# Transposing attention probabilities and MLP tokens: by TensorE, or by VectorE in blocks and a trip through DRAM

## The chip, the cores and the metric

The kernel runs on one core of one Trainium2 chip. The metric is the device time of one execution in microseconds; the time of a kernel is the median of its runs. One further execution is taken by the hardware profiler, and every duration of a single instruction comes from that one.

## The reference

The input `x` holds 8 images of 192 channels and 64 x 64 pixels, in float32. Two layers follow each other; all weights are float32 too.

```python
# layer 0, on tokens (one per pixel, 192 channels)
shortcut = layer_norm(tokens)
q, k, v = windows_of_8x8(shortcut) @ qkv_w.T + qkv_b       # 6 heads of 32
attn = l2n(q) @ l2n(k).T * temperature                     # 64 x 64 for each window and head
attn = where(attn >= 16th_largest_of_the_row, attn, -100)
out = softmax(attn + relative_position_bias) @ v
x2 = shortcut + (out @ proj_w.T + proj_b)
x2 = x2 + gelu(layer_norm(x2) @ fc1_w.T + fc1_b) @ fc2_w.T + fc2_b     # 192 -> 768 -> 192

# layer 1
xf = fft2(layer_norm over channels)                        # 64 x 64, for each channel
h = gelu([xf.real, xf.imag] @ fc1_w.T + fc1_b) @ fc2_w.T + fc2_b       # 2 -> 16 -> 2
x = x + ifft2(h).real
out = x + gelu(layer_norm(x) @ mlp1_w.T + mlp1_b) @ mlp2_w.T + mlp2_b  # 192 -> 768 -> 192
```

## The kernel before

**Tiling.** An image is cut into 8 bands of 512 pixels (8 rows). Every band passes `front` (load, first norm, q, k and v), `attention` twice (two halves of four windows each), and `back` (projection, residual, first MLP). When all 8 bands of an image are in, its 192 channels go in 12 groups of 16 through the Fourier part: `forward`, two of `pointwise`, and `inverse`. Then `leave` takes each band through the second MLP, turns it back into channels and stores it. That gives 128 halves of attention and 128 MLPs: 64 in `back` (tiles whose names end in `_b`) and 64 in `leave` (`_d`).

**The two transposes.** A matmul contracts over partitions. In `attention`, the probabilities `s` come out with queries on the partitions, and the product with `v` (line 928) contracts over keys. So six 128x128 blocks of `s` are transposed by TensorE into PSUM (line 903) and evicted into `at` by ScalarE or VectorE (`copy`, line 819). In `mlp`, the normalised tokens `xa` have pixels on the partitions, and the first product (`mh`, lines 589 and 602) contracts over channels. So six transposes (`to_channels`, lines 541 and 546) go into `lc`, which is evicted into `hn`. The product `mh` is passed through GELU into `h` (line 573), and the second product `mo` (line 635) brings it back to tokens, to which VectorE adds the residual (`xy` line 996, `zt` line 1212).

**What sets the order.** The kernel is written as generators that yield steps, `op(engine, weight, ...)`. The function `issue` plays them against a clock of its own for each engine: a step has a weight (one unit stands for about 10 ns), may need buffers from a ring (`get`) and gives them back (`put`), and costs extra where TensorE changes its tile shape or ScalarE its function (`change`). At each turn `issue` takes the step that can begin first, weighed by how late its task is in the image. The instructions are recorded in that order, and each engine runs its own in that order, waiting on semaphores. So the order on every engine is fixed when the program is built, and rests on the weights. The streams are: one `front`, three attentions, two `back`, one `forward`, two `pointwise`, one `inverse` and two `leave` under way at a time; the second layer of an image runs beside the first layer of the next one. The ring `ps` has 4 buffers of two PSUM banks, `att` 5 buffers of 768 columns, `hn` 2, `ot` 1.

**SyncE** issues nearly all transfers, each band's loads of `xin` (lines 192 and 195) and its stores of `z` (lines 1226 and 1228), on one queue and in order. In the kernel before, the loop gives it no weight.

Of the kernel before, what the change touches and what calls it, by code (L numbers as in the profile page):

```python
# [8 lines left out]
FP = mybir.dt.float32  # L9
# [6 lines left out]
C = 192  # L16
CA = 128
HC = 96
HW = 64
BAND = 512  # L20
# [8 lines left out]
def op(engine, weight, mode=None, get="", put="", after=None, done=None, put_too=""):  # L29
    return engine, weight, mode, get.split(), (put + " " + put_too).split(), after, done  # L30


def issue(streams, units):

    change = {"pe": 20, "act": 130, "dve": 0, "pool": 0}
    clock = {e: 0 for e in change}
    mode = {e: None for e in change}  # L40
    units = {name: [0] * n for name, n in units.items()}
    events = {}
    live = []

    def advance(task, value):
        try:
            found = task["gen"].send(value)
            while not isinstance(found, tuple):

                new = dict(task, gen=found, queue=None)  # L50
                live.append(new)
                advance(new, None)
                found = task["gen"].send(None)
            task["op"] = found
        except StopIteration:
            live.remove(task)
            if task["queue"] is not None:
                start(task["queue"])

    def start(queue):  # L60
        if queue[0]:
            gen, place = queue[0].pop(0)
            task = {"gen": gen, "queue": queue, "urgency": 360 * place, "last": (None, 0)}
            queue[1] += 1
            task["order"] = (queue[1], len(live), place)
            live.append(task)
            advance(task, None)

    for tasks, width in streams:
        queue = [list(tasks), 0]  # L70
        for _ in range(width):
            start(queue)
    while live:
        best, ready = {}, {}
        for task in live:
            engines, weights, kind, get, put, after, done = task["op"]
            if isinstance(engines, str):
                engines, weights = (engines,), (weights,)
            free = 0
            deps = [task["last"]] if after is None else after  # L80
            deps = [d if d[0] is None or d[0] in change else events.get(d) for d in deps]
            if any(d is None for d in deps):
                continue
            short = False
            for name in set(get):
                n = get.count(name)
                if len(units[name]) < n:
                    short = True
                    break
                free = max(free, sorted(units[name])[n - 1])  # L90
            if short:
                continue
            found = []
            for engine, weight in zip(engines, weights):
                begin = max(clock[engine], free)
                for source, end in deps:
                    if source is not None and source != engine:
                        end += 30 if source == "pe" else 15
                    begin = max(begin, end)
                new = kind and mode[engine] and kind != mode[engine]  # L100
                cost = change[engine] if new else 0
                found.append((begin + cost + weight, engine, begin, cost, task, weight))

            _, engine, *rest = min(found, key=lambda f: f[0] + 40 * (f[1] == "dve"))
            ready.setdefault(engine, []).append((engine, *rest))
        for engine, found in ready.items():
            first = min(begin + cost for _, begin, cost, *_ in found) + 15
            best[engine] = min(
                [
                    (  # L110
                        begin + cost + task["urgency"] - 100 * ("ps" in task["op"][4]),
                        task["order"],
                        f,
                    )
                    for f in found
                    for _, begin, cost, task, _ in [f]
                    if begin <= first
                ],
                key=lambda v: v[:2],
            )  # L120
        choice = min(best.values(), key=lambda v: (v[2][1], v[:2]))[2]
        engine, begin, change_cost, task, weight = choice
        _, _, kind, get, put, after, done = task["op"]
        for name in get:
            units[name].remove(min(units[name]))
        end = begin + change_cost + weight
        clock[engine] = end
        if kind:
            mode[engine] = kind
        for name in put:  # L130
            units[name].append(end + 15)
        task["last"] = (engine, end)
        if done:
            events[done] = (engine, end)
        advance(task, (engine, end))
# [3 lines left out]
def kernel(  # L139
# [28 lines left out]
    def psum(name):  # L168
        return psp.tile([128, 2, 512], FP, tag="ps", name=name)


    ATT_BUFS, H_BUFS, XT_BUFS = 5, 7, 4
    units = dict(
        ps=4, xt=XT_BUFS, xn=1, qk=1, vv=2, att=ATT_BUFS, qkt=1, sm=2, ot=1, hn=2, xa=2,
        h=H_BUFS, xf=1, fa=1, fz=2, fo=1, xy=2,
    )

    xins = {}
# [371 lines left out]
    def flat(name):  # L550
        return psum(name).rearrange("p k n -> p (k n)")

    def mlp(src, nm, w1, fc1_bias, w2, then=None):

        mv = yield from statistics(src, nm)
        yield op("pool", 0, get="xa")
# [1 line left out]
        last = yield from normalized(to, pair, src, mv, nm)  # L558
        if then is not None:
            yield then()  # L560
        yield op("pe", 66, "full", get="ps hn", put="xa", after=last)
        pc = flat(f"lc_{nm}")
        to_channels(pc, pair, to)
        done = yield op(EITHER, (80, 96), put="ps")
        hn = strip("hn", 2, f"hn_{nm}")
        copy(done, hn, pc[:, :ROW])
        hs = []

        def gelu(fp, ph, last):
            yield op("act", 138, "gelu", put="ps", after=[last], done=("gelu", nm, fp))  # L570
            h = sb.tile([128, 2, BAND], FP, tag="h", name=f"h_{nm}_{fp}", bufs=H_BUFS)
            for k in range(2):
                nc.scalar.activation(  # L573
                    h[:, k].rearrange("p (t n) -> p t n", t=2),
                    ph[:, :, k * HALF : (k + 1) * HALF],
                    AF.Gelu,
                    bias=fc1_bias[:, 2 * fp + k : 2 * fp + k + 1],
                )
            hs.append(h)
# [240 lines left out]

    EITHER = ("act", "dve")

    def attention(b, i, hb):

        nm = f"{b}_{i}_{hb}"
# [69 lines left out]
        yield op("pool", 150, put="sm")  # L895
        nc.gpsimd.tensor_tensor(s, s, row(rsum), ALU.mult)  # L896

        yield op("pe", 65, "full", get="ps att", put="att")
        pt = flat(f"at_{nm}")
        for h3 in range(3):  # L900
            for p in range(2):
                k = 2 * h3 + p
                nc.tensor.transpose(
                    pt[:, k * 128 : (k + 1) * 128],
                    s[:, h3, 2 * p : 2 * p + 2, :].rearrange("p w k -> p (w k)"),
                    ident,
                )
        moved = yield op(EITHER, (80, 96), put="ps")
        at = sb.tile([128, 3, 2, 128], FP, tag="att", name=f"at_{nm}", bufs=ATT_BUFS)
        copy(moved, at.rearrange("p h a t -> p (h a t)"), pt[:, :ROW])  # L910

        if hb == 0:
            yield op("pe", 53, "v", get="ps ot", put="att", after=[moved, ("vv", b, i)], done=("ot", b, i))
            ots[b, i] = strip("ot", 1, f"ot_{nm}")
        else:
            yield op("pe", 53, "v", get="ps", put="att " + held[b, i][1], after=[moved, ("ot", b, i)])
        po = psum(f"po_{nm}")
        for p in range(2):
            for h in range(6):
# [5 lines left out]
                for to, col, q0, n in places:  # L925
                    for w2 in range(2):
                        rows = slice(64 * w2, 64 * w2 + 64)
                        nc.tensor.matmul(  # L928
                            po[to : to + 32, w2, col : col + n],
                            vv[rows, p, h * 32 : h * 32 + 32],  # L930
                            at[rows, h3, p, c * 64 + q0 : c * 64 + q0 + n],
                            start=True,
                            stop=True,
                        )
# [11 lines left out]
    def back(b, i):  # L946
# [36 lines left out]
            nc.gpsimd.tensor_tensor(xt, xt, bias2, ALU.add)  # L983

        pair = lambda t, j: xt[:, j, t * C : (t + 1) * C]
        acc, last = yield from mlp(pair, f"b{nm}", wfc1, fcb[:, 0, :], wfc2, biased)
        ready = [last, ("biased", b, i)]
        yield op("dve", 98, put="ps xt", get="xy" if i == 0 else "", after=ready)
        if i == 0:
            xys[b] = (  # L990
                sb.tile([128, 2, 2, 8, C], FP, tag="xy", name=f"xy_{b}", bufs=2),
# [203 lines left out]
    def leave(b, j):  # L1195
# [3 lines left out]
        if j == 0:  # L1199
# [4 lines left out]
        yield op("pool", 0, after=blocks + [("dc", b), ("mlp", 1)])  # L1204
        xy = xys[b][0]
        acc, last = yield from mlp(
            lambda t, q: xy[:, t, q, j, :], f"d{nm}", wmlp[0], fcb[:, 1, :], wmlp[1]
        )
        left[b] -= 1
        yield op("dve", 98, get="xa", put="ps xy" if left[b] == 0 else "ps")  # L1210
# [127 lines left out]
```

## Time and profile before

| | |
|---|---|
| median of 3 runs | 4787.68 us (4782.2 to 4788.69) |
| the profiled execution: its own time | 4796.72 us |
| the profiled execution: its span | 4794.9 us |
| TensorE busy | 4545.6 us, 95% of the span |
| TensorE weight loads | 3633.2 us, 76% |
| ScalarE busy | 2663.2 us, 56% |
| VectorE busy | 2532.9 us, 53% |
| GpSimd busy | 2364.8 us, 49% |
| queue of SyncE | 53,454 packets, 54.68 MB, 3.8% of 16 DMA engines |

The span is the time between the first and the last instruction that the profiler saw. A float32 matmul stands as two records in the trace, a transpose as one. The records of matmuls overlap: the mean duration of one is a latency, and the busy time of a group counts each moment once. In a row of a group, the last part is the time that the engine sat idle just before its instructions, and what ended most of it. The granted clock is the share of its full clock that TensorE was given; its mean was 0.979. In the page's names PE is TensorE, DVE VectorE, ACT ScalarE, POOL GpSimd and SP SyncE, and SPq is SyncE's issue of a transfer.

### The profile page before, as it was taken

What the parts mean: (1) busy time and instruction counts of PE and PEld (TensorE: products, weight loads), DVE (VectorE), ACT (ScalarE), POOL (GpSimd) and SP (SyncE); (2) the same over time, 40 slices, a digit from 0 to 9 for tenths busy, and PEclk for the clock granted to TensorE, in tenths of its full rate; (3) what the DMA queues carried; (4) which work ended last, traced back from release to release, by engine and by line L of the source; (5) the groups of instructions that cost most, each with busy time, mean ns of one, the idle gap of its engine ahead of it and who ended that gap; (6) DMA issues with size and microseconds to landing.
All of it is one profiled execution on the core that took longest, in us unless ns stands there. A gap on an engine that the chain in (4) does not pass through costs nothing.

```text
span 4794.9 us, 143562 instructions
## 1 busy us (share of the span) xinstructions
PE 4545.6 (95%) x61898; PEld 3633.2 (76%) x61898; DVE 2532.9 (53%) x10479; ACT 2663.2 (56%) x3896; POOL 2364.8 (49%) x2189
## 2 busy tenths in 40 slices
PE   6787999999999999999999999999999999999989
PEld 4676777877778776887778876788767887778768
DVE  6776656455664567454655546645556454662111
ACT  4455666446664656555655556545566456553553
POOL 6677455445544446454555545536455455451100
PEclk8888999999999999999999999999999999999999
DMA  2000000000000000000000000000000000000000
GB/s 57 11 8 12 6 9 9 21 18 6 12 9 18 18 9 9 11 21 15 6 9 17 18 12 9 9 18 15 12 9 9 24 12 9 6 5 17 9 5 24
DMA packets 54100, 63.87 MB, mean 13 GB/s; under 512 B 17583, under 2 KB 36218, under 8 KB 53466
## 3 DMA queue, kind: packets, MB, share of 16 engines
q1 hardware_dynamic: 53454, 54.68, 3.8%
q8 instruction: 487, 7.98, 0.7%
q14 instruction: 147, 1.20, 0.1%
q10 hardware_dynamic: 12, 0.00, 0.0%
HBM read 29.29 MB, written 25.17 MB: 11 GB/s over the span
## 4 chain that ended last, share of the span: by engine, by line
PE 78%; POOL 7%; DVE 7%; ACT 5%; issue 2%; SPq 0%; DMA 0%; ACTq 0%; POOLq 0%; DVEq 0%
PE mo_d L635 10%; PE mo_b L635 10%; PE mh_d L589 7%; PE fh L1099 7%; PE fo L1126 6%; PE mh_b L589 6%; PE mh_d L602 4%; PE mh_b L602 3%; POOL nrm L738 3%; PE pq L754 3%; ACT fh L1082 3%; PE pp L956 2%; PE fy L1174 2%; PE po L928 2%; PE fb L1147 2%
## 5 line engine op out<-in xcount | busy, mean ns | idle before, releaser
L1082 ACT ACTIVATE fh<-fh,ab 128x1024 f32<-128x1024 f32 x768 | 813.1, 1111 | 395.1 <-PE fh L1099 392.5
L738 POOL TENSOR_TENSOR nrm<-nrm,mhalf 128x24 f32<-128x24 f32 x128 | 558.3, 4362 | 10.7
L886 POOL TENSOR_TENSOR s<-s,top 128x768 f32<-128x768 f32 x128 | 191.6, 1496 | 724.1 <-DVE s L883 445.0
L635 PE MATMUL mo_b<-wfc,h_b 128*128 128x192 f32 x3072 | 522.4, 328 | 0.3 <-ACT fh L1082 0.2
L635 PE MATMUL mo_d<-wmlp,h_d 128*128 128x192 f32 x3072 | 516.0, 327 | 1.3 <-ACT fh L1082 1.3
L635 PEld LDWEIGHTS mo_b<-wfc,h_b 128*128 128x128 f32 x3072 | 500.4, 191 | 10.0 <-issue 3.7
L635 PEld LDWEIGHTS mo_d<-wmlp,h_d 128*128 128x128 f32 x3072 | 498.1, 190 | 11.4 <-issue 5.8
L1099 PE MATMUL fh<-fz,w1p 32*128 32x248 f32 (+1 forms) x6144 | 461.0, 404 | 20.3 <-ACT fh L1082 14.7
L1099 PEld LDWEIGHTS fh<-fz,w1p 32*128 32x128 f32 x6144 | 291.2, 186 | 149.2 <-issue 77.6
L1126 PE MATMUL fo<-fh,w2p 128*32 128x264 f32 (+1 forms) x6144 | 380.0, 383 | 7.8 <-ACT fh L1082 5.6
L589 PE MATMUL mh_b<-hn_b,wfc_a 128*128 128x256 f32 x1536 | 376.5, 392 | 10.8 <-ACT xt L819 4.8
L589 PE MATMUL mh_d<-hn_d,wmlp_a 128*128 128x256 f32 x1536 | 366.5, 386 | 0.5 <-ACT hn_d L819 0.3
L573 ACT ACTIVATE h_d<-mh_d,fcb 128x512 f32<-128x512 f32 x384 | 241.1, 686 | 214.7 <-PE mh_d L602 179.3
L589 PEld LDWEIGHTS mh_b<-hn_b,wfc_a 128*128 128x128 f32 x1536 | 283.7, 192 | 76.9 <-issue 25.8
L589 PEld LDWEIGHTS mh_d<-hn_d,wmlp_a 128*128 128x128 f32 x1536 | 283.0, 191 | 56.2 <-issue 19.1
L896 POOL TENSOR_TENSOR s<-s,rsum 128x768 f32<-128x768 f32 x128 | 200.0, 1567 | 236.6 <-DVE rsum L894 191.1
L876 DVE MATCH_REPLACE8 s<-top,s 128x64 f32<-128x64 f32 x1536 | 309.6, 209 | 0.0
L1126 PEld LDWEIGHTS fo<-fh,w2p 128*32 128x32 f32 x6144 | 185.3, 110 | 158.8 <-issue 30.2
L874 DVE MAX8 top<-s 128x8 f32<-128x64 f32 x1536 | 256.7, 208 | 51.0 <-ACT s L819 50.6
L1212 DVE TENSOR_TENSOR zt<-mo_d,xy 128x768 f32<-128x768 f32 x64 | 61.2, 957 | 413.1 <-PE mo_d L635 306.4
L878 DVE MAX8 top<-s 128x8 f32<-128x64 f32 x1536 | 265.3, 214 | 0.0
L573 ACT ACTIVATE h_b<-mh_b,fcb 128x512 f32<-128x512 f32 x384 | 241.3, 691 | 38.5 <-PE mh_b L602 27.6
(218 smaller groups left out, 8763.7 us busy)
## 6 DMA issues: line engine op xcount, KB each, us to landing
xin<-in_x SPq DMA_DIRECT2D x64, 256.0 KB
out<-z SPq DMA_DIRECT2D x64, 256.0 KB
xin<-in_x SPq DMA_DIRECT2D x128, 64.0 KB
out<-z SPq DMA_DIRECT2D x128, 64.0 KB
wfc<-in_wfc SPq DMA_DIRECT2D x1, 576.0 KB
wmlp<-in_wmlp SPq DMA_DIRECT2D x1, 576.0 KB
wfc_a<-in_wfc SPq DMA_DIRECT2D x1, 384.0 KB
wfc_b<-in_wfc SPq DMA_DIRECT2D x2, 192.0 KB
```

The lines of the kernel that those rows point to most:

```text
L573: nc.scalar.activation(h[:, k].rearrange("p (t n) -> p t n", t=2), ph[:, :, k * HALF : (k + 1) * HALF], AF.Gelu, bias=fc1_bias[:, 2 * fp + ...
L589: nc.tensor.matmul(ph[:, t, k * HALF : (k + 1) * HALF], w1[0][:, f], hn[:, t * HALF : (t + 1) * HALF], start=(first and k == 0), stop=not ...
L602: nc.tensor.matmul(ph[:, t, k * HALF : (k + 1) * HALF], w1[1][rows, f], hn[rows, BAND:ROW], start=(first and k == 0), stop=not first, skip ...
L635: nc.tensor.matmul(acc[:, j, t * C : (t + 1) * C], hs[f // 2][:, f % 2, q * 128 : (q + 1) * 128], w2[:, f, ORDER[t]], start=(f == 0 and t ...
L738: nc.gpsimd.tensor_tensor(nf, nf, mhalf[:, :24], ALU.pow)
L874: nc.vector.max(best[:, 0:8], of)
L876: nc.vector.match_replace(s2, best[:, 0:8], of, -3.0e38)
L878: nc.vector.max(best[:, 8:16], s2)
L896: nc.gpsimd.tensor_tensor(s, s, row(rsum), ALU.mult)
L1082: nc.scalar.activation(hs[hf, k], ph, AF.Gelu, bias=ab[:, 0:1])
L1099: nc.tensor.matmul(phs[k // 2][:, k % 2, cols], w1p[i][rows, hf].rearrange("p h v -> p (h v)"), fz[rows, :] if rhs is None else zu[rows, : ...
L1126: nc.tensor.matmul(po[rows, :] if i == 0 else pou[rows, :, 1 : U - 1], w2p[i][:, hf].rearrange("p a v -> p (a v)"), hs[hf, k // 2][:, k % ...
```

## The change

Probabilities of images 1 to 7 (112 of 128 halves) and the tokens of all MLPs but the 8 of image 0's `back` (120 of 128) no longer go through TensorE and PSUM. VectorE transposes 32x32 blocks within SBUF, in two instructions for a half of attention and three for an MLP. SyncE then writes the result to a DRAM tile in four transfers, one for each quarter of the partitions, so that the blocks land in their places, and reads it back in one transfer (`at`) or three (`hn`). A read waits for the landing of its writes. `hn` then holds its tokens in another order, and GELU writes `h` with an access pattern that puts them right. The product with `v` reads its columns in runs of 32. The planner gets an engine `sp` with weights of its own and arrival times, three DRAM buffers for each kind of turn, a second `ot`, and a condition between the bands of an image (`xy`). As the plan is made anew, the order of the instructions changes on all engines.

```diff
-    change = {"pe": 20, "act": 130, "dve": 0, "pool": 0}
+    change = {"pe": 20, "act": 130, "dve": 0, "pool": 0, "sp": 0}
+    arrives = {"pe": 30, "sp": 210}
...
-                        end += 30 if source == "pe" else 15
+                        end += arrives.get(source, 15)
...
-            units[name].append(end + 15)
+            units[name].append(end + (150 if engine == "sp" else 15))
...
-    ATT_BUFS, H_BUFS, XT_BUFS = 5, 7, 4
+    ATT_BUFS, H_BUFS, XT_BUFS, TURN_BUFS = 5, 7, 4, 3
...
-    def mlp(src, nm, w1, fc1_bias, w2, then=None):
+    def mlp(src, nm, w1, fc1_bias, w2, by_dma, then=None):
...
+        if by_dma:
+            ready = yield op("dve", 115, get="att rows", put="xa", after=last)
+            turned = sb.tile([128, 6, 2, 2, 32], FP, tag="att", name=f"lt_{nm}", bufs=ATT_BUFS)
+            whole = to.rearrange("p j (g k) -> p j g k", k=32)
+            for t, g, c, n in ((0, 0, 0, 6), (1, 6, 4, 2), (1, 8, 0, 4)):
+                nc.vector.transpose(
+                    turned[:, c : c + n, t].rearrange("p g j k -> p j g k"),
+                    whole[:, :, g : g + n],
+                )
+            yield op("sp", 220, put="att")
+            rows = dram.tile([C, 4, 128], FP, tag="rows", name=f"lr_{nm}", bufs=TURN_BUFS)
+            into = rows.rearrange("(g c) q n -> q c g n", c=32)
+            for q in range(4):
+                part = turned[32 * q : 32 * q + 32].rearrange("p g t j k -> p g (t j k)")
+                nc.sync.dma_start(into[q], part)
+            yield op("sp", 130, get="hn", put="rows")
+            hn = strip("hn", 2, f"hn_{nm}")
+            nc.sync.dma_start(hn[:, :BAND], rows[:CA].rearrange("c q n -> c (q n)"))
+            for t in range(2):
+                nc.sync.dma_start(
+                    hn[64 * t : 64 * t + 64, BAND:],
+                    rows[CA:, 2 * t : 2 * t + 2].rearrange("c q n -> c (q n)"),
+                )
+        else:
...
+                if by_dma:
+                    to = h[:, k].rearrange("p (g t q n) -> p t q g n", g=4, t=2, q=2)
+                    of = of.rearrange("p t (q g n) -> p t q g n", q=2, g=4)
...
+    def turned_by_dma(s, nm):
+        yield op("dve", 108, get="att turn", put="att")
+        tt = sb.tile([128, 4, 2, 3, 32], FP, tag="att", name=f"tt_{nm}", bufs=ATT_BUFS)
+        for p in range(2):
+            nc.vector.transpose(
+                tt[:, :, p].rearrange("q g h k -> q h g k"),
+                s[:, :, 2 * p : 2 * p + 2, :].rearrange("q h w (e k) -> q h (w e) k", k=32),
+            )
+        yield op("sp", 220, put="att")
+        rows = dram.tile([128, 4, 192], FP, tag="at", name=f"ar_{nm}", bufs=TURN_BUFS)
+        to = rows.rearrange("(g k) c n -> c k g n", k=32)
+        for c in range(4):
+            part = tt[32 * c : 32 * c + 32].rearrange("q g p h k -> q g (p h k)")
+            nc.sync.dma_start(to[c], part)
+        moved = yield op("sp", 45, get="att", put="turn")
+        at = sb.tile([128, 4, 2, 3, 32], FP, tag="att", name=f"at_{nm}", bufs=ATT_BUFS)
+        nc.sync.dma_start(
+            at.rearrange("q c p h k -> q (c p h k)"), rows.rearrange("r c n -> r (c n)")
+        )
...
-        yield op("pe", 65, "full", get="ps att", put="att")
...
+        if b == 0:
+            moved, keys = yield from turned_by_pe(s, nm)
+        else:
+            moved, keys = yield from turned_by_dma(s, nm)
...
-                            at[rows, h3, p, c * 64 + q0 : c * 64 + q0 + n],
+                            keys(rows, h3, p, c * 64 + q0, n),
...
-        acc, last = yield from mlp(pair, f"b{nm}", wfc1, fcb[:, 0, :], wfc2, biased)
+        acc, last = yield from mlp(pair, f"b{nm}", wfc1, fcb[:, 0, :], wfc2, b > 0, biased)
...
+        if i > 0:
+            ready.append(("xy", b))
```

## The prediction

> **What bounds the kernel now.** First the busy time of the engines and the chain that ended last, from the page of the profiled run.
>
> ```profile
> span 4794.9 us, 143562 instructions
> ...
> PE 4545.6 (95%) x61898; PEld 3633.2 (76%) x61898; DVE 2532.9 (53%) x10479; ACT 2663.2 (56%) x3896; POOL 2364.8 (49%) x2189
> ...
> PE 78%; POOL 7%; DVE 7%; ACT 5%; issue 2%; SPq 0%; DMA 0%; ACTq 0%; POOLq 0%; DVEq 0%
> ```
>
> TensorE is busy for 95% of the span and carries 78% of the chain; nobody else is above 56%. So work taken from TensorE shortens the run, unless TensorE waits for what replaces it. Its idle time is 4794.9 − 4545.6 = 249 us. The windows say where that lies.
>
> ```profile
> 0.00:240.00 240.00, 172.19 (x1854) 131.19 (x1854) 169.97 (x735) 107.37 (x185) 159.07 (x143) 0.83 0.15 34
> 240.00:480.00 240.00, 198.41 (x2459) 160.77 (x2458) 165.71 (x710) 126.52 (x207) 176.04 (x151) 0.87 0.03 10
> ...
> 1680.00:1920.00 240.00, 225.96 (x4035) 169.06 (x4035) 161.01 (x631) 145.11 (x191) 135.15 (x115) 0.99 0.03 9
> 1920.00:2160.00 240.00, 238.05 (x2405) 204.53 (x2402) 119.23 (x524) 132.53 (x219) 120.18 (x127) 1.00 0.05 16
> ```
>
> The columns after the length are TensorE, its weight loads, VectorE, ScalarE, GpSimd, the granted clock, the DMA share and GB/s. The first two windows, which are image 0, leave 68 + 42 = 110 us idle at a granted clock of 0.83 and 0.87; later ones leave 2 to 14 us. Image 0 keeps its transposes on TensorE, so the change acts where TensorE has hardly a gap. Third, the groups it touches, shapes kept apart:
>
> ```profile
> L903 PE MATMUL at<-ident,s 128*128 128x128 f32 x768 | 112.5, 287 | 61.3 <-POOL s L896 56.7 <-ACT fh L1082 2.2 <-POOL xf L1022 1.7
> L541 PE MATMUL lc_b<-ident,xa_b 128*128 128x128 f32 x256 | 43.0, 286 | 8.2 <-ACT xa_b L525 6.3 <-ACT fh L1082 0.8
> L541 PE MATMUL lc_d<-ident,xa_d 128*128 128x128 f32 x256 | 41.5, 284 | 6.3 <-ACT xa_d L525 5.9
> ...
> L836 DVE STREAM_TRANSPOSE qkt<-qk 128x768 f32<-128x768 f32 x128 | 125.4, 979 | 61.4 <-PE s L846 45.7 <-issue 12.6 <-POOL xf L1023 0.4
> ```
>
> The 287 ns of one transpose is its latency; they overlap. What counts is how far a group of six moves TensorE on, and the timeline of its instructions tells that:
>
> ```profile
> 2007.62 0.66 PE L541 MATMUL lc_d<-ident,xa_d 128*128 128x128 f32 x4
> 2008.11 0.38 PE L546 MATMUL lc_d<-ident,xa_d 128*128 128x128 f32 x2
> 2008.33 7.97 PE L635 MATMUL mo_d<-wmlp,h_d 128*128 128x192 f32 x48
> ...
> 2017.86 0.60 PE L541 MATMUL pz<-ident,zt 128*128 128x128 f32 x4
> 2018.29 0.38 PE L546 MATMUL pz<-ident,zt 128*128 128x128 f32 x2
> 2018.51 1.46 PE L754 MATMUL pq<-wqkv_a,xn 128*128 128x384 f32 x4
> ```
>
> From start to the next start a group takes 0.71 and 0.65 us; I take 0.68.
>
> **What is removed.** 7 x 16 = 112 groups for probabilities and 56 + 64 = 120 for tokens: 232 x 0.68 = 158 us of TensorE (151 to 165 by the two starts). The waits ahead of these groups I put at nothing: they wait for the operand, and the new path waits for the same operand. Nor is much there: in the window 480 to 4320 us the wait of `at` for `s` is 5.2 us of the 56.7, the rest belongs to image 0. The PSUM evictions go too: ScalarE's `at` 115 x 799 ns, `hn_d` 61 x 799 ns and `hn_b` 41 x 798 ns, all of the second and 7/8 of the others. Those 80 + 49 + 29 = 158 us of ScalarE lie beside TensorE and count nothing.
>
> **What VectorE gets.** `qkt`, 768 elements a partition, takes 979 ns. Copies of 768, 256 and 128 columns from PSUM take 957, 422 and 279 ns, so an instruction costs some 0.13 us before its elements. Two blocks of 384: 0.98 + 0.13 = 1.11 us; three pieces with 768 in all: 0.98 + 0.26 = 1.24 us. Sum 112 x 1.11 + 120 x 1.24 = 273 us, less some 35 evictions of 0.957 us: +240 us. VectorE goes from 53% to about 58%, and in its fullest later window (161 of 240) by another 13 us. Cover: TensorE's work. Costing nothing on the path is my value; its upper end is rival D. VectorE now waits for GpSimd's last product into `s`, with other halves' `max` work and the `fz`, `xy`, `zt` steps queued behind; before, only TensorE waited there. GELU's output is written in runs of 32: 0, because the permuted `xn` copy of 512 columns takes 584 ns where the plain `fb` copy of 512 takes 585. The attention product with 64 columns reads them in two runs of 32: 0 as well, since `fy`, which reads 256 columns in runs of 32, takes 427 and 383 ns a record and `mh`, of the same shape and without runs, 393 to 396; 10 ns on each of 3584 records (7/8 of 4096) would be 36 us, an upper end.
>
> **What SyncE and the DMA get.** 112 x 5 + 120 x 7 = 1400 transfers on the one queue that also holds 192 loads of `xin` and 192 stores of `z`. Added packets: 112 x (512 + 128) + 120 x (768 + 256) = 194,560. The page has 53,454 packets at 3.8% of 16 engines, so these take about 14%: bandwidth is no limit. Latency is. Its rows:
>
> ```profile
> 65.56 1.31 SPq L433 DMA_DIRECT2D frow<-in_fwd  x4
> 68.31 1.89 SPq L435 DMA_DIRECT2D frow<-frow  x3
> ...
> 2041.47 0.35 SPq L192 DMA_DIRECT2D xin<-in_x  x1
> 2041.87 1.14 SPq L195 DMA_DIRECT2D xin<-in_x  x2
> ```
>
> Issues cost 0.35 us for the first and 0.55 for each further one. `frow<-frow` waits for the landing of `frow<-in_fwd`, as the new reads wait for their writes: its last issue starts at 66.5, so a landing took 1.8 us. At the end the last `z` issue starts at 4792.06 and the span ends at 4794.9: under 2.8. I take 2.1, nearer the chain that is the same shape. A turn of probabilities: VectorE 1.1, four writes until the last starts 1.45, landing 2.1, read 2.1, semaphores 0.25: 7.0 us. A turn of tokens has three reads, the last starting 0.9 later, and 0.1 more on VectorE: 8.0. By 1.8 they are 6.4 and 7.4, by 2.8 8.4 and 9.4. The old way, transposes, eviction and semaphores, took about 2.
>
> Does TensorE have that much else to do? In the changed program's order I counted its work between each turn's VectorE instruction and the turn's first reader on TensorE, priced by start to start from the timeline (a half of mo 3.95 us, mh 1.82 and 0.98, fh 1.08, fo 1.97, transposes 0.68). Quartiles for probabilities: 4.8, 6.1, 7.6 us; for tokens: 7.0, 10.6, 17.2. Short of the need are 74 of 112 and 37 of 120, by 156 and 95 us: 251 us in all (191 and 432 at the two ends, with 93 and 146 turns short). That is too much for two reasons. The step that TensorE is in at that moment is not counted: the kernel before hands TensorE 3205 steps (a step is one `op`), 4795 / 3205 = 1.5 us each, half of it for 111 turns is 83, so 168 stay. And stalls don't add: three attentions and four MLPs are under way, a stall at one covers the others, and the 249 us of idle time that are there take some. I take two thirds: 112 us. Lower end a third of (191 − 70): 40; upper end all of (432 − 110): 322.
>
> **Sum.** −158 + 112 = −46 us on the profiled run's own time, 4796.7 (its span 4794.9 and 1.8 around it): 4751. That run lies 9 us above the median of 4787.68, so 4742 us.
>
> Two rules speak against it. By the Trainium skill, "VectorE: DVE Perf Modes", section Rules for kernel authors, a 128x128 transpose belongs on TensorE where PSUM is a possible destination: by that rule the change only loses, and the sum would be above 4788. The rows differ, 0.68 us of the engine that bounds against idle time elsewhere, and I go by them. The clock has its row in the tail, where TensorE waits 5.5 us for image 7's tokens:
>
> ```profile
> 4643.22 1.34 PE L541 MATMUL lc_d<-ident,xa_d 128*128 128x128 f32 x4 [5.48 <-ACT xa_d L525]
> ...
> 4646.95 3.62 PE L589 MATMUL mh_d<-hn_d,wmlp_a 128*128 128x256 f32 x8
> ...
> 4657.46 1.99 PE L589 MATMUL mh_d<-hn_d,wmlp_a 128*128 128x256 f32 x8
> ```
>
> After the gap the same steps take twice their time, some 4 us lost in all. Short stalls of 1 to 2 us show no such loss in the rows, so I charge none. By the skill's "TensorE: Matmul & The Clock Gate", section What's actually happening, the clock halves after an idle window of about 3.4 us: if a third of the 111 short turns crossed that, 37 x 4 = 148 us would come on top and the change would lose.
>
> **The rivals.** **A, the forecast**: about half the saving is lost in waits; 4715 to 4790; chance 0.52. **B, the cover is nearly whole**: stalls of 40 us, 4788 − 118 = 4670; for it that TensorE is never the one ahead in a 95% busy run, against it the quartiles; 0.25. **C, slower: the trip through DRAM becomes TensorE's wait**. Place: the first attention product and the first `mh` behind each turn, on an in-order SyncE where one turn's read waits for its landing while the next turn's writes and a `z` store stand behind. Price: 251 to 322 us of stalls, 4788 + 93 to + 164 = 4881 to 4952, less by what overlaps; it decides from 158 / 232 = 0.68 us of stall per turn; 0.20. **D, VectorE ends it**: the 240 us delay `fz`, `xy`, `zt` in its queue by more than TensorE has other work; it decides from the saved 158 us on, and at 170 us gives 4800; against it 58%; 0.03. That the transposes aren't gone is excluded: the changed order has 16 groups of `at`, 8 of `lc_b`, none of `lc_d`.
>
> **How the numbers follow.** 0.2%, 9.6 us, is what a measurement can tell from no change. Faster: all of B and 0.45 of A, 0.70; within: 0.05 of A, 0.03 of C, 0.01 of D, 0.09; slower: 0.02 of A, 0.17 of C, 0.02 of D, 0.21. The range reaches from B's end, 4665, to 4830, where C's overlaps leave it half of its low price; about 0.08 below and 0.12 above are left out.
>
> **What would show it.** Right: TensorE's busy time down by about 160 to 220 us (the page counts the tails), its idle time up by about 110, with waits of `po`, `mh_b` and `mh_d` for DMA at 1 to 2 us each, half of the probabilities' turns among them; VectorE +240; DMA share near 18%; GELU still at 690 ns. Wrong: idle unchanged (B), stalls over 3 us with the clock falling (C), landings far from 2.1 us, or waits of `fz` and `zt` for VectorE (D).

## The result and the profile after

The changed kernel takes 4827.04 us (4825.89 to 4827.91) against 4788.18: a ratio of 1.0082 with a 95% interval of 1.0069 to 1.0096. It is slower by 39 us, where 46 us faster was forecast. The page of the changed kernel, the lines that answer to those of before:

```profile
span 4826.1 us, 143829 instructions
...
PE 4441.2 (92%) x60506; PEld 3512.4 (73%) x60506; DVE 2695.8 (56%) x10965; ACT 2542.1 (53%) x3769; POOL 2358.2 (49%) x2188
...
q1 hardware_dynamic: 270414, 237.22, 17.7%
...
PE 66%; DVE 10%; POOL 7%; DMA 7%; ACT 5%; issue 3%; SPq 2%; DVEq 0%; ACTq 0%; POOLq 0%
```

TensorE lost 61,898 − 60,506 = 1392 instructions, the 232 groups of six. Its busy time fell by 104 us only, where the sum had 158, and its idle time rose from 249 to 385 us: −104 + 136 = +31 us of span, the difference of the two profiled runs. VectorE is at 56% and the DMA engines at 17.7%: neither is full. DMA and SyncE now hold 9% of the chain, where they had nothing. The head of TensorE's list of waits (engine and line, what it waited for: us in total, times, longest):

```profile
PE po L997 <- DMA at<-ar: 99.1, 52, 5.7
PE at L863 <- POOL s L974: 48.6, 7, 12.1
PE s L924 <- DVE qkt L914: 32.1, 12, 9.0
PE mh_d L622 <- DMA hn_d<-lr_d: 23.1, 9, 13.3
PE mh_b L622 <- DMA hn_b<-lr_b: 20.3, 11, 4.6
```

The first, fourth and fifth did not exist before and make 142.5 us. One of these waits, seen on three engines by their timelines (VectorE, SyncE, TensorE):

```profile
1527.96 1.04 DVE L880 STREAM_TRANSPOSE tt<-s 128x384 f32<-128x384 f32 x2
```

```profile
1526.00 0.34 SPq L583 DMA_DIRECT2D hn_b<-lr_b  x1
1526.38 1.10 SPq L585 DMA_DIRECT2D hn_b<-lr_b  x2
1527.58 0.52 SPq L1304 DMA_DIRECT2D out<-z  x1
1528.15 1.13 SPq L1306 DMA_DIRECT2D out<-z  x2
1529.32 2.96 SPq L889 DMA_DIRECT2D ar<-tt  x4
1533.83 0.34 SPq L892 DMA_DIRECT2D at<-ar  x1
```

```profile
1532.53 1.45 PE L787 MATMUL pq<-wqkv_a,xn 128*128 128x384 f32 x4
1537.34 0.80 PE L997 MATMUL po<-at,vv 64*32 64x64 f32 x64 [3.36 <-DMA at<-ar]
1538.07 3.59 PE L635 MATMUL mh_b<-hn_b,wfc_b 64*128 64x256 f32 x16
...
1682.01 2.00 PE L635 MATMUL mh_b<-hn_b,wfc_b 64*128 64x256 f32 x16
```

VectorE is done at 1529.0, SyncE's first write goes out at 1529.32 behind six transfers of other work, its four issues take 2.96 us where the median of the 112 turns is 1.78, the read is issued at 1533.83, and TensorE starts at 1537.34: 9.4 us for the turn, 3.36 of them idle. The last two lines show a second price. The `mh_b` step behind the wait takes 3.59 us; the same 16 instructions take 2.00 elsewhere. TensorE's clock had been halved: from 1538.1 to 1541.7 us the granted clock is 0.53. Over the run, the mean granted clock went from 0.979 to 0.963: the time that was not granted rose from 4794.9 x 0.021 = 101 to 4826.1 x 0.037 = 179 us.

### The profile page after: what moved, and what is told of

Read it like the earlier page. It is cut to its first block, busy times and chain, and to the rows that moved or that the text cites. A ratio compares the mean times of both kernels' runs of the same rounds, so it can differ in the third digit from the quotient of the medians.

```text
span 4826.1 us, 143829 instructions
## 1 busy us (share of the span) xinstructions
PE 4441.2 (92%) x60506; PEld 3512.4 (73%) x60506; DVE 2695.8 (56%) x10965; ACT 2542.1 (53%) x3769; POOL 2358.2 (49%) x2188
## 3 DMA queue, kind: packets, MB, share of 16 engines
q1 hardware_dynamic: 270414, 237.22, 17.7%
## 4 chain that ended last, share of the span: by engine, by line
PE 66%; DVE 10%; POOL 7%; DMA 7%; ACT 5%; issue 3%; SPq 2%; DVEq 0%; ACTq 0%; POOLq 0%
PE mo_d L668 8%; PE mo_b L668 7%; PE mh_b L622 7%; PE mh_d L622 6%; PE fh L1177 6%; PE fo L1204 6%; PE mh_b L635 3%; PE mh_d L635 3%; PE pq L787 3%; POOL nrm L771 3%; DMA at<-ar 3%; ACT fh L1160 2%; DMA ar<-tt 2%; PE fy L1252 2%; PE fb L1225 2%
## 5 line engine op out<-in xcount | busy, mean ns | idle before, releaser
L1177 PE MATMUL fh<-fz,w1p 32*128 32x264 f32 (+1 forms) x6144 | 468.6, 410 | 14.7 <-ACT fh L1160 6.5
L622 PE MATMUL mh_b<-hn_b,wfc_a 128*128 128x256 f32 x1536 | 391.3, 402 | 34.8 <-DMA hn_b<-lr_b 20.3
L1204 PE MATMUL fo<-fh,w2p 128*32 128x264 f32 (+1 forms) x6144 | 390.9, 389 | 5.7 <-ACT fh L1160 5.5
```

The lines of the kernel that those rows point to most:

```text
L622: nc.tensor.matmul(ph[:, t, k * HALF : (k + 1) * HALF], w1[0][:, f], hn[:, t * HALF : (t + 1) * HALF], start=(first and k == 0), stop=not ...
L1177: nc.tensor.matmul(phs[k // 2][:, k % 2, cols], w1p[i][rows, hf].rearrange("p h v -> p (h v)"), fz[rows, :] if rhs is None else zu[rows, : ...
L1204: nc.tensor.matmul(po[rows, :] if i == 0 else pou[rows, :, 1 : U - 1], w2p[i][:, hf].rearrange("p a v -> p (a v)"), hs[hf, k // 2][:, k % ...
```

## The experiments

All times are compared with the kernel before on the same chip. Theory 1: the loss is the trip through DRAM, as waits for landings and as the clock that they cost. Theory 2: it is VectorE's added work. This is the ledger of the profiled runs, one for each kernel; the ratio is from all runs. Idle is the span less TensorE's busy time, "waits" are TensorE's waits for `at` and `hn` from DRAM, "ungranted" is the span times one minus the clock.

| kernel (figures for a turn's writes and arrival in the plan) | ratio to before, interval | PE busy | idle | waits | ungranted |
|---|---|---|---|---|---|
| before | 1 | 4546 | 249 | 0 | 101 |
| after (2.2 and 2.1) | 1.0082 [1.0069, 1.0096] | 4441 | 385 | 142 | 179 |
| e1 probabilities only | 1.0172 [1.0155, 1.0189] | 4526 | 355 | 119 | 166 |
| e2 tokens only | 0.9959 [0.9946, 0.9971] | 4473 | 297 | 46 | 105 |
| e3 both (3.5 and 2.7) | 0.9926 [0.9914, 0.9938] | 4426 | 328 | 78 | 143 |
| e4 as after, no own landing | 0.9912 [0.9898, 0.9926] | 4423 | 316 | 78 | 147 |
| e5 both (4.5 and 3.3) | 0.9831 [0.9818, 0.9845] | 4404 | 303 | 53 | 113 |
| e6 tokens only (3.5 and 2.1) | 0.9951 [0.9938, 0.9963] | 4462 | 304 | 21 | 119 |
| e7 as e3, no own landing | 0.9849 [0.9836, 0.9863] | 4408 | 311 | 38 | 118 |
| e9 both (5.6 and 3.9) | 0.9932 [0.9920, 0.9945] | 4434 | 325 | 49 | 148 |
| e10 neither | 0.9977 [0.9968, 0.9986] | 4539 | 237 | 0 | 81 |
| e11 probabilities only (4.5 and 3.3) | 0.9866 [0.9853, 0.9880] | 4469 | 254 | 11 | 99 |
| e12 as e5, no own landing | 0.9806 [0.9792, 0.9819] | 4406 | 283 | 35 | 113 |

**Each half alone.** Probabilities alone:

```diff
-        acc, last = yield from mlp(pair, f"b{nm}", wfc1, fcb[:, 0, :], wfc2, b > 0, biased)
+        acc, last = yield from mlp(pair, f"b{nm}", wfc1, fcb[:, 0, :], wfc2, False, biased)
...
-            lambda t, q: xy[:, t, q, j, :], f"d{nm}", wmlp[0], fcb[:, 1, :], wmlp[1], True
+            lambda t, q: xy[:, t, q, j, :], f"d{nm}", wmlp[0], fcb[:, 1, :], wmlp[1], False
```

> Only the probabilities take the new way; all 128 MLPs stay on TensorE. Theory 1, the landing: the changed kernel lost because TensorE waited for landings (99 us at po, 43 us at mh) and because those waits cost it clock (0.979 to 0.963, some 78 us of full-clock time in the span). Then this half carries most of the loss: -112 x 0.68 = -76, +99 of waits, +50 of clock: 4788 + 73 or less where the plan covers more, 4820 to 4860, and po's wait for DMA stays at 80 to 120 us. Theory 2, VectorE: its added work of 163 us in an in-order queue delays others; the loss of 39 us goes by its share, 123 of the measured additions: about 4800 to 4815.

Tokens alone:

```diff
-        if b == 0:
+        if True:
             moved, keys = yield from turned_by_pe(s, nm)
```

> Only the tokens take the new way; all probabilities stay on TensorE. Theory 1, the landing: -120 x 0.68 = -82 us, +43 of waits, +20 to 28 of clock: faster than before by 5 to 25 us, 4763 to 4783; waits of mh for DMA 30 to 60 us. Theory 2, VectorE: slower than before by about half of the loss, 4800 to 4815.

4870 us and 4771 us. The tokens came as theory 1 had them in time and waits, though the clock cost them 4 us more than before and not 20 to 28; the probabilities came on the same side but 10 us above its range. Theory 2 had both between 4800 and 4815. The quartiles of the forecast's count point the same way: half of the probabilities' turns had under 6.1 us of other work in front of them, half of the tokens' over 10.6. The halves don't add up: +82 and −20 make +62, and together they cost 39.

**The planner's figures.** The same work, another order; only which of ScalarE and VectorE evicts a tile follows the plan, by some tens of copies:

```diff
-    arrives = {"pe": 30, "sp": 210}
+    arrives = {"pe": 30, "sp": 270}
...
-            yield op("sp", 220, put="att")
+            yield op("sp", 350, put="att")
```

with the same 350 in `turned_by_dma`.

> The changed kernel, and only the planner's figures differ: a turn's writes are planned at 3.5 us in place of 2.2 and the arrival at 2.7 in place of 2.1, near what the trace shows (write issue to read issue 3.4, read issue to po 3.1 or more). The instructions are the same, their order is not. Theory 1, the landing: TensorE's waits for DMA fall from 142 us to under 60, the clock is above 0.97, and the time is 4720 to 4770, below before. Theory 2, VectorE: as much VectorE work in as many instructions, so within 15 us of the changed kernel, 4812 to 4842.

4756 us, 71 us under the changed kernel with VectorE at 2689 us against 2696: theory 2, which had 4812 to 4842, falls. VectorE's queue is in another order too, so the stricter test is e4 below, where the order stays. The waits went to 78 us, not to under 60, and the clock to 0.970. Then further, 450 and 330:

> The changed kernel with the planner's figures raised further: writes 4.5 us and arrival 3.3, about 1.1 us over the trace for the writes. Theory 1, the landing: TensorE's waits for DMA fall from the 78 us that are left with 3.5 and 2.7 to under 40, and the time is 4735 to 4757. Rival, the plan's limit: there is no more other work to put in front of a turn, so what leaves the waits for DMA comes back as waits for the engines in front of the turn, and the time is 4755 to 4785.

4708.93 us (4706.67 to 4710.78), better than theory 1 asked for, though the waits at 53 us are above its 40. The rival is out. And 560 and 390:

> The changed kernel with 5.6 us for the writes and 3.9 for the arrival in the plan. Theory 1, the landing: 2.2 and 2.1 gave 4827, 3.5 and 2.7 gave 4756, 4.5 and 3.3 gave 4709; now nearly every turn is covered, so little is left to win and the planner's own waiting begins to cost: 4700 to 4730, waits for DMA under 35 us. Rival, luck of the order (any new order moves the time by some tens of us either way): anywhere from 4690 to 4830.

4757 us: outside theory 1's range. The waits for DMA are no more than in e5, yet idle time is 22 us and ungranted time 35 us higher, in waits for other engines. So the figures don't act smoothly. With nearly the same sum of waits for DMA, the order made 48 us.

**A control for the order:**

```diff
-        if b == 0:
+        if True:
             moved, keys = yield from turned_by_pe(s, nm)
```

together with the two edits of the first experiment, so that every transpose is back on TensorE.

> All else of the change (a second ot buffer, the condition between bands, the planner's new terms), but every transpose on TensorE as before. Theory 1: these edits are not what moved the time, 4775 to 4800. Rival, luck of the order: more than 25 us away from 4790 on either side, which would be the size by which a new order alone moves this kernel.

4778 us, 11 us better than before. So the side edits are not the loss, nor is a new plan as such; this is one order, and e9 against e5 shows that two can lie 48 us apart.

**Probabilities alone with the better figures** (450 and 330):

> Only the probabilities take the new way, with 4.5 us for the writes and 3.3 for the arrival in the plan. Theory 1, the landing: with the figures of 2.2 and 2.1 this half took 4870 with 119 us of po's waits for DMA; now these fall to under 45 and the time to 4730 to 4775, below before. Rival, the probabilities don't gain in any order (the chain of attention is what is too long): 4790 or more.

4723 us, 7 us below theory 1's range, with 11 us of waits. This pair is the cleanest of the study: e1 and e11 hold the same work in two orders, e1 first.

```profile
PE 4526.0 (93%) x61226; PEld 3596.9 (74%) x61226; DVE 2614.1 (54%) x10688; ACT 2588.8 (53%) x3806; POOL 2367.4 (49%) x2190
...
PE po L997 <- DMA at<-ar: 119.4, 64, 6.3
```

```profile
PE 4468.8 (95%) x61226; PEld 3555.2 (75%) x61226; DVE 2578.8 (55%) x10636; ACT 2611.7 (55%) x3859; POOL 2386.1 (51%) x2203
...
PE po L997 <- DMA at<-ar: 11.2, 14, 1.4
```

TensorE's 61,226 instructions are busy for 57 us less in e11, at a clock of 0.979 against 0.966, and idle for 101 us less, while the waits for `at` fell by 108. Against before, at the same clock of 0.979, e11's busy time fell by 77 us: 112 groups of 0.68 are 76. So the price of a group was right. That what the changed kernel lacks of its 158 is clock can be read from the trace's records of the granted clock, which hold only full and half: half of TensorE's busy time in the half-clock stretches, the work lost there, is 67 us before, 67 in e11, 122 in e1 and 127 in the changed kernel.

**Tokens alone with better figures** (350 for the writes):

> Only the tokens take the new way, and the planner has 3.5 us for their writes (arrival 2.1 as it was). Theory 1, the landing: the 46 us of mh's waits for DMA fall to under 25 and the time goes from 4771 to 4745 to 4765. Rival, the plan's limit: 4765 to 4780, the waits reappear elsewhere.

4767 us against 4771 for e2. The waits fell from 46 to 21, the time hardly: a wait for `s` by the old `at` transposes in image 0 and after grew instead (108 us in e6, 63 in e2). The rival, with 4765 to 4780, has this one.

**Without the landing of one's own writes.** The orders of the changed kernel, e3 and e5, with

```diff
+        own = rows
...
         moved = yield op("sp", 45, get="att", put="turn")
+        rows = earlier.get("turn", own)
+        earlier["turn"] = own
```

and the same in `mlp`, and eight DRAM buffers of each kind. Each read takes the rows of the turn before, so the kernel leaves out the wait for its own writes and computes other values; its transfers and its order stay.

> The changed kernel in the same planned order, with all its transfers, but each read takes the rows of an earlier turn, so it need not wait for its own writes to land (the values are those of another turn). Theory 1, the landing: a turn is shorter by about 1.6 us, TensorE's waits for DMA fall to 30 to 70 us, the clock is above 0.97, and the time is 4710 to 4770. Theory 2, VectorE: nothing of VectorE's work has changed, 4812 to 4842. A third, the traffic (190 MB on the DMA engines and SyncE's queue): also 4812 to 4842, with waits of po and mh for DMA that stay.

> The order of the kernel with 3.5 and 2.7 us in the plan, and each read takes an earlier turn's rows, so that a turn is about 2 us shorter than it is planned (the values are those of another turn). Theory 1, the landing: hardly any wait for DMA is left (under 30 us), the clock is 0.973 or more, and the time is 4710 to 4740: what is then missing from the 158 us lies in the order itself. Rival: waits for DMA are not what holds the kernel with the better plan, within 10 us of 4756.

> The order of the kernel with 4.5 and 3.3 us in the plan, and each read takes an earlier turn's rows, so that it does not wait for its own writes (the values are those of another turn). Theory 1, the landing: of the waits for DMA only 48 us were left, so little more can be won: 4685 to 4710. Rival, the landings still hold much, through SyncE's queue and not through the waits that are seen: below 4680.

4747, 4719 and 4694 us. What shortening the turn is worth falls with the waits that the order had left: 1.7% in the changed kernel (142 us of waits), 0.8% in e3 (78), 0.25% in e5 (53). Traffic and VectorE's work are those of the kernel that each is compared with. For e4 and the changed kernel, VectorE's 10,965 instructions are the same:

```profile
PE 4423.2 (93%) x60506; PEld 3502.3 (74%) x60506; DVE 2686.7 (57%) x10965; ACT 2543.0 (54%) x3769; POOL 2360.2 (50%) x2188
...
PE po L1004 <- DMA at<-ar: 58.2, 35, 3.5
```

So neither VectorE's work nor the traffic makes the loss by itself; whether the traffic lengthens a landing was not tested. In e4 78 us of waits stayed, 8 more than the top of the range that was expected, and the clock was 0.969 where above 0.97 was expected; most of the waits are at `po`: from the read's issue to its reader it is 3 us and more. In e7 38 us stayed where under 30 were expected. The times of all three lie in theory 1's ranges.

**Short stalls and the clock**, by themselves: no part of the reference, only bursts of 36 matmuls with a stall behind each.

```python
            for k in range(BURST):        # 36
                nc.tensor.matmul(pt[:, 0:192], weight, data[:, 0:192], start=True, stop=True)
...
            weight = sb.tile([128, 128], FP, tag="weight", name=f"w_{seg}_{rep}", bufs=2)
            nc.vector.tensor_copy(weight, pt[:, 0:128])
            for k in range(cols):         # 0, 1, 2, 3, 5, 7, 10 copies
                nc.vector.tensor_copy(weight, ident)
```

> Nothing of the reference is computed. Eight stretches of 16 bursts of 36 float32 matmuls of 192 columns (about 12 us of TensorE each); in the first nothing stands between the bursts, in the others the next burst's weight is copied by VectorE from the burst before, with 0, 1, 2, 3, 5, 7 and 10 more copies, so that TensorE stalls by about 0.6 to 3 us once in 12 us. Theory 1, short stalls cost clock: the granted clock is 1.00 for stalls under 1 us and drops to 0.9 or less where stalls pass some 1.2 to 1.5 us, well under 3.4 us of idle in a row. Rival, only an idle stretch of 3 us or more costs clock: 1.00 up to the last stretch or two.

The timeline of TensorE at 5, 7 and 10 copies (start, length of a burst, idle before it):

```profile
1024.92 11.94 PE L53 MATMUL pt<-data,w 128*128 128x192 f32 x72 [1.79 <-DVE w L60]
1038.64 11.94 PE L53 MATMUL pt<-data,w 128*128 128x192 f32 x72 [1.78 <-DVE w L60]
...
1319.56 11.94 PE L53 MATMUL pt<-data,w 128*128 128x192 f32 x72 [2.30 <-DVE w L60]
1333.81 13.62 PE L53 MATMUL pt<-data,w 128*128 128x192 f32 x72 [2.31 <-DVE w L60]
...
1498.78 13.62 PE L53 MATMUL pt<-data,w 128*128 128x192 f32 x72 [3.09 <-DVE w L60]
1515.49 13.62 PE L53 MATMUL pt<-data,w 128*128 128x192 f32 x72 [3.09 <-DVE w L60]
```

By the windows (the first number behind the counts is the granted clock):

```profile
1015.00:1220.00 205.00, 178.26 (x1077) 174.27 (x1076) 21.40 (x90) 0.00 (x0) 1.00 0.00 1
1225.00:1470.00 245.00, 206.33 (x1190) 201.81 (x1189) 31.51 (x134) 0.00 (x0) 0.96 0.00 1
1475.00:1725.00 250.00, 203.22 (x1115) 198.93 (x1114) 38.82 (x167) 0.00 (x0) 0.92 0.00 1
```

Up to 1.79 us a stall cost nothing but itself: every burst is 11.94 or 11.97 us long. At 2.31 us 6 of 16 bursts were 13.62 long, at 3.09 us 11 of 15: 1.68 us more, a stretch of about 3.4 us at half the clock. The clock records say why only some: the half-clock stretches are 3.41 us long and begin on one grid of 3.41 us. Every stall between bursts of which 1.99 us or more fell into one step of the grid was followed by such a stretch, and no stall of which 1.98 us or less did was. Theory 1's threshold of 1.2 to 1.5 us was too low here, the rival's 3 us too high. In the kernel itself, whose matmuls are of many shapes, the border lies lower: between 480 and 4320 us of the changed kernel, every step of the grid that began at full clock and held 1.8 us of idle time or more was followed by half the clock, and some with 1.3 us.

## Why the prediction was wrong

- **What was removed** was right in its price: 232 x 0.68 = 158 us. e11 shows it for the probabilities: 77 us of busy time gone at the same clock, 76 by the sum.
- **The stalls**: the step "I take two thirds: 112 us" gave too little, by 24 us; idle time rose by 136 and the waits for landings are 142.5. The full 168 would have been 32 too many. The waits themselves are much as forecast: 52 of the 112 turns of probabilities, 1.9 us each on average. One reason for the shortfall stands a step earlier: the landing of the 384 KB read was taken at 2.1 us like the others. In the trace a waiting `po` starts 3.4 us behind the issue of its read by the median of the 52 (3.5 above, 1533.83 to 1537.34), so a turn of probabilities is nearer 8 us than 7.0. The write side was right: 1.3 us from the first to the last issue and 2.0 until the read's issue, medians of the 112 turns in the trace, against 1.45 and 2.1.
- **The clock** is the step that turned the sign: "Short stalls of 1 to 2 us show no such loss in the rows, so I charge none." Charged at nothing, it was 78 us of ungranted time, of which 54 are what TensorE's busy time lacks of the sum (158 − 104). By the clock records the work lost at half clock rose from 67 to 127 us, by 60. The rows behind the step, one long gap in the tail, were too few, and the trace of the kernel before held others: between 480 and 4320 us it has 12 half-clock stretches, 41 us in all, each behind 1.2 to 2.2 us of idle time within the 3.4 us before it. The changed kernel has 31 there, 181 us, and in 21 of them a wait for a landing is the larger part of that idle time. By the Trainium skill, "TensorE: Matmul & The Clock Gate", section What's actually happening, the clock halves after an idle window of about 3.4 us. The half-clock stretch in e8 has that length, but the stall that brings it on was shorter, 2.31 us.
- Together: −158 + 136 + 54 = +32 us, and the spans differ by 31. This closes by construction, as 54 is what was left over; the check is the 60 of the clock records. With the stalls alone, −158 + 136 = −22, the change would have won.
- **The rival C** had the direction and the place, not the price: 39 us where it had 93 to 164. It needed more than 158 us of stalls, and they were 142. The clock, which the forecast names as a sign of C but which is not in C's price, made the difference.
- **VectorE**: 1.10 us a turn of probabilities, as forecast. Its busy time rose by 163 us, not 240: the records of the new transposes add up to 271 us, as forecast, but 57 us of copies left it where 34 were counted, and the records overlap more. It holds 10% of the chain after 7%; e4, with the same VectorE work in the same order, gains 80 us. The skill's rule in "VectorE: DVE Perf Modes", section Rules for kernel authors, that a 128x128 transpose belongs on TensorE, agrees with the changed kernel and disagrees with e5, where the same work moved off TensorE wins 1.7%.
- **GELU** in runs of 32 cost nothing (690 and 686 ns), and `po`'s records went from 231 and 199 to 238 and 203 ns, at a lower clock.
- **Still open**: why e9's order is 48 us worse than e5's with the same waits for DMA, and why the probabilities alone cost more than both halves together. Orders differ everywhere, and no run here takes that apart. So the size of e5's gain may be partly that of a lucky order; that a covered turn gains is shown by e3, e5, e9 and e11.
- **Two small readings** of the forecast are off and change nothing: the later windows leave 1.2 to 14 us of idle time, and 18 in the last, not 2 to 14; and the last store leaves 2.84 us, not under 2.8.

## What to carry to other kernels

When an engine at 95% hands work to a path with a longer latency, the saving is real only where the order of its instructions has that latency covered: here the same work took from 4709 to 4827 us, by two figures in a static planner. Measure every leg of the new path at its own size before the order is fixed, the read as well as the write. And price a stall of TensorE at more than its length: from 2 us in dense bursts, and from little over 1 us of idle time within 3.4 us in these kernels, it can take half of the next 3.4 us too.

## What the runs showed of the hardware

- A dependence from a write to a read through DRAM, issued by SyncE, took about 6.7 us by the medians: 1.3 us from the first to the last of four issues, 2.0 us until the read could be issued, 3.4 us from there to its waiting reader for 384 KB.
- A single stall in 12 us of dense float32 matmuls cost no clock up to 1.79 us, half of about 3.4 us in 6 of 16 cases at 2.31 us, and in 11 of 15 at 3.09 us. What counted was the part of the stall within one step of a fixed 3.41 us grid: 1.99 us or more cost clock, 1.98 or less did not.
- The added DMA traffic, from 3.8% to 17.7% of the DMA engines, does not by itself bring a loss: e4, e7 and e12 carry all of it and are 0.9% to 1.9% faster than the kernel before.
